# Closing an attention's output rows elsewhere in the schedule, and loading its keys through ScalarE's queue

## The chip, the core and the metric

The kernel runs on one core of a Trainium2 chip (trn2), in one launch. The metric is device time in microseconds, the median of several runs. Engines are named as in the profile: PE is TensorE's matmuls and PEld its weight loads, DVE is VectorE, ACT is ScalarE, POOL is GpSimd and SP is SyncE, which issues DMAs. Each engine takes its own instructions in program order.

## What is computed

The input x is (2, 2048, 512) in float32, with one condition vector per batch. Two layers follow each other. The first is a conditioned state-space block (norm and modulation, a diagonal scan along the length, a gate, a second norm, a feed-forward net 512 to 2048 to 512 with gelu, gated residuals). The second is an attention block; the change lies in it and just ahead of it:

```python
def _sln(h, w, ln_g, ln_b, Wg, bg, Wb, bb):
    mu = jnp.mean(h, axis=-1, keepdims=True)
    var = jnp.mean((h - mu) ** 2, axis=-1, keepdims=True)
    ln = (h - mu) / jnp.sqrt(var + EPS) * ln_g + ln_b
    gamma = (w @ Wg.T + bg)[:, None, :]
    beta = (w @ Wb.T + bb)[:, None, :]
    return gamma * ln + beta
...
h = _sln(hidden, w, ...)
q, k, v = (h @ Wqkv.T + bqkv) in 16 heads of 32
att = jax.nn.softmax(q @ k.T, axis=-1) / D ** 0.5
h1 = (att @ v) @ Wp.T + bp + hidden
h2 = _sln(h1, w, ...)
return h2 + h1
```

The last line is computed per row as y * g_row + (h1 + t_row), where y = (h1 - mean) * rstd, and g_row and t_row hold the condition's gamma and beta with ln_g and ln_b folded in.

## The kernel before

**Stages.** From 0 to about 1380 us the first layer runs over eight chunks of 512 rows (two batches of four), with the attention's norm, heads and values of the chunk before placed between. From 1380 to 1488 us lies the transition: at_norm (the attention's norm) of the last chunk, at_values of the last two chunks and at_heads of the last one, handed out from the list `left` (line 681), beside the first score work of the attention. In it, one PSUM bank (`ones`) serves all value tiles one after the other: at_values (line 541) does four matmuls into `pv`, DVE adds the bias row (line 548), which frees the bank, and SP stores the tile.

**Attention** runs from 1488 to 3513 us: 64 blocks, each a batch, a pair of heads and a chunk of 512 queries. A block has NP = 8 periods, numbered through j = 0 to 511. In each period 16 key tiles' worth of a block advances by two: ten tiles' scores are kept in SBUF 15 periods ahead (`keep`, lines 758 to 767: scores on PE, a copy on ACT, a running maximum on DVE), and six are made afresh in the period (`make`, 812 to 817: scores on PE, the shift added by DVE). `across` (769) takes the maximum of those six on PE and DVE. `turn_run` (785) turns the running maximum at positions 2 and 4 of a block's periods, and `spread` (795), at position 5, sends the negated maxima to DRAM (`flat`, 802) and reads them back on all partitions (`shift`, 804), for the block that begins three periods later. `take_off` (808, on POOL) adds the shift to kept scores a period ahead; `exponentials` (819, on ACT) run twice a period; `weighted` (824) multiplies the exponentials of the period before by the values.

**The order** is written out by hand: the loop at 1113 issues, for each j, first what `due` holds for j (run_due), then make, across, the first exponentials, the keeps, the pieces from `left`, the second exponentials, take_off for j + 1 and weighted for j - 1. Since every engine takes its instructions in this order, a place in the loop is a place in each engine's queue. `after(j, what, ...)` at 1055 enters a step. The schedule (1060 to 1103) enters, for block n: load_k (723, eight DMAs of 256 KB per pair of heads, i.e. per four blocks, at 8n - 27, which is position 5 of a block, the same due list as a spread and ahead of it), load_q (732, eight DMAs, position 3), load_v (742, two DMAs, 8n - 9).

**Closing the rows.** The output rows of a batch are closed in 16 tiles `qt` of 128 rows. Batch 0's are closed beside batch 1's attention, in blocks 34 to 57, a tile in every one and a half blocks, with all steps of a tile in fixed positions: last_rows (854) once, at block 34; then per tile fetch (874, six DMAs on SP) at position 3, divide (889, POOL) at position 5, project (894) in four groups at 6, 7, 0 and 1, moments (909, DVE) behind the last group, deviation (917, DVE, three Newton steps to 1/sqrt(var) in a PSUM tile `dev`) at the start of position 2, last_norm (937) at 3, close (946) at 4. last_norm has ACT write z = h * scale + shift to PSUM (941) and DVE multiply by g_row (943); close has POOL add t_row to h (949) and h to y (950), and SP store y (951). Twelve tiles of the last batch (LB) go through the same functions at the end (positions by `k = j + 3 + 2 * t`), and the last four rows' tiles through end_fetch to end_last (959 to 1027).

Of the kernel before, what the change touches and what calls it, by code (L numbers as in the profile page):

```python
# [8 lines left out]
F32 = mybir.dt.float32  # L9
# [4 lines left out]
AF = mybir.ActivationFunctionType  # L14
ALU = mybir.AluOpType
# [4 lines left out]
P = 128  # L20
# [19 lines left out]
def tile_s5_block_then_sln_attention(  # L40
# [21 lines left out]
    nc = tc.nc  # L62
    NB, L, D = x.shape
    KC = D // P
    CH = 512
# [4 lines left out]
    NG = D // P  # L70
# [5 lines left out]
    small = ctx.enter_context(tc.tile_pool(name="small", bufs=2))  # L76
# [26 lines left out]
    kd = [dpool.tile([2, D, L], F32, name=f"kd_{b}") for b in range(NB)]  # L103
# [98 lines left out]
    order = [(b, c) for b in range(NB) for c in range(NCH)]  # L202
# [59 lines left out]
    for q in range(4):  # L262
        f = FC // 4
# [58 lines left out]
    half, odd, turn, sign, even = col("half"), col("odd"), col("turn"), col("sign"), col("even")  # L322
# [64 lines left out]
    gate, last, bus, hs, pos, hids = {}, {}, {}, {}, {}, {}  # L387
# [127 lines left out]
    def at_norm(b, c):  # L515
        normalised(b, c)
        xc = xt.pop((b, c))
        for t in range(TT):
            nc.gpsimd.tensor_tensor(xc[:, t, :], xc[:, t, :], bp_row, ALU.add)
        nc.sync.dma_start(x2[b][c * CH : (c + 1) * CH, :].rearrange("(t p) d -> p t d", p=P), xc)  # L520
# [17 lines left out]
        nc.sync.dma_start(dst[0, g * P : (g + 1) * P, at], hi.bitcast(F32))  # L538
        nc.sync.dma_start(dst[1, g * P : (g + 1) * P, at], lo.bitcast(F32))

    def at_values(b, c, t):
        pv = ones.tile([P, CH], F32, name="pv")
        for k in range(KC):
            nc.tensor.matmul(
                pv, fts[b, c][:, k, t * P : (t + 1) * P], wv[:, k, :], start=k == 0, stop=k == KC - 1
            )
        vt = work1.tile([P, D], F32, name="vt", tag="gated")
        nc.vector.tensor_add(vt, pv, bv_row)
        nc.sync.dma_start(vd[b][c * CH + t * P : c * CH + (t + 1) * P, :], vt)


# [54 lines left out]
    for name, src in (("wk", w_kT), ("wq", w_qT), ("wv", w_vT)):  # L606
        w = wlate.tile([P, KC, D], F32, name=name)
# [3 lines left out]
    bv_row = wlate.tile([P, D], F32, name="bv_row")  # L611
# [14 lines left out]
    for i, now in enumerate(order):  # L626

        due = {(f, h): [] for f in range(FC + 1) for h in range(2)}
# [34 lines left out]
        def run_due(at):  # L663
            for what, *args in due[at]:
                what(*args)
# [15 lines left out]
    left = []  # L681
    for chunk in order[-2:]:
        for t in range(TT):
            left.append((at_values, *chunk, t))
    for j in range(2 * KC):
        left.insert(TT + j, (at_heads, *order[-1], j))
    for k in range(KC):
# [16 lines left out]
    ps = ctx.enter_context(tc.tile_pool(name="ps2", bufs=1, space=PSUM, side="right"))  # L704
# [6 lines left out]
    u, v = NPAIR - 2, NPAIR - 1  # L711
# [11 lines left out]
    def load_k(i):  # L723
        b, p = pairs[i]
        for e in range(2):
            f = slice(HD * (2 * p + e), HD * (2 * p + e + 1))
            ks = kpools[i % 2].tile([P, L], HALF, name="ks")
            for r in range(4):
                nc.sync.dma_start(ks[32 * r : 32 * r + 32, :].bitcast(F32), kd[b][r % 2, f, :])
            kst[i, e] = ks  # L730

    def load_q(n):
# [161 lines left out]
    def project(b, qt, groups=tuple(range(NG))):  # L894

        o4, h, *py = held[b, qt]
        if py:
            py = py[0]
        elif len(groups) == NG:
            py = ps.tile([P, 2, CH], F32, name="py2", tag="m")[:, 0, :]  # L900
        else:
            py = ps.tile([P, CH], F32, name="py", tag="pt")
        for g in groups:
            nc.tensor.matmul(py, o4[:, g, :], wp[:, g, :], start=g == 0, stop=g == NG - 1)
        held[b, qt] = o4, h, py
        if groups[-1] == NG - 1:
            held[b, qt] = h, moments(h, py)

    def moments(h, py):
        nc.vector.tensor_add(h, py, h)  # L910
        st = small.tile([P, 6], F32, name="st3")
        nc.vector.bn_stats(st, h)
        mv = small.tile([P, 2], F32, name="mv3", bufs=4)
        nc.vector.bn_aggr(mv, st)
        return mv

    def deviation(b, qt):

        h, mv = held[b, qt]
        w = ps.tile([P, 3], F32, name="dev", tag="pt")  # L920
        v, c = w[:, 0:1], w[:, 1:2]
        half = small.tile([P, 1], F32, name="half3")
        y = small.tile([P, 1], F32, name="scale3", bufs=3)
        nc.vector.tensor_scalar(v, mv[:, 1:2], EPS, None, ALU.add)
        nc.vector.tensor_scalar(half, v, -0.5, None, ALU.mult)
        nc.vector.tensor_scalar(
            y.bitcast(I32), v.bitcast(I32), -0.5, float(0x5F3759DF), ALU.mult, ALU.add
        )
        for _ in range(3):
            nc.vector.tensor_scalar(c, y, y, half, ALU.mult, ALU.mult)  # L930
            nc.vector.scalar_tensor_tensor(y, c, 1.5, y, ALU.add, ALU.mult)
        shift = small.tile([P, 1], F32, name="shift3", bufs=3)
        nc.vector.tensor_scalar(c, mv[:, 0:1], y, None, ALU.mult)
        nc.vector.tensor_scalar(shift, c, -1.0, None, ALU.mult)
        held[b, qt] = h, y, shift

    def last_norm(b, qt):

        h, scale, shift = held[b, qt]
        z = ps.tile([P, CH], F32, name="z", tag="pt")  # L940
        nc.scalar.activation(z, h, AF.Identity, bias=shift, scale=scale)
        y = work.tile([P, D], F32, name="y")
        nc.vector.tensor_tensor(y, z, ending[b][0], ALU.mult)  # L943
        held[b, qt] = h, y

    def close(b, qt):

        h, y = held.pop((b, qt))
        nc.gpsimd.tensor_tensor(h, h, ending[b][1], ALU.add)  # L949
        nc.gpsimd.tensor_tensor(y, y, h, ALU.add)  # L950
        nc.sync.dma_start(out[b, qt * P : (qt + 1) * P, :], y)


# [79 lines left out]
    AHEAD = 15  # L1033
# [18 lines left out]
    due = {}  # L1052

    def after(j, what, *args):
        due.setdefault(j, []).append((what, args))

    N = len(blocks)
    FIRST = -AHEAD - 8
    OPEN = -4
    for i, n in enumerate(opens):  # L1060
        free = NP * (max(m for m in range(N) if pair_of[m] == i - 2) + 1) if i > 1 else FIRST
        after(max(free, NP * n - AHEAD - 12), load_k, i)
        after(max(OPEN, NP * n - 9), load_v, i)
# [5 lines left out]
    for b in range(NB):  # L1069
        for c in range(NQ):  # L1070
            j = NP * (blocks.index((b, NPAIR - 1, c)) + 1) + 1
            if (b, c) == (LB, LC):
                most = slice(0, NH - 4)
                j = NP * (N - 1) - 2
                after(j - 3, fetch_sums, b, c, most)
                after(j - 1, invert, b, c, most)
                after(j + 1, end_fetch)
                after(NP * (N - 1) + 3, end_fetch_more)
                for g in range(NG - 1):
                    after(j + 5 + g, end_divide, g)  # L1080
                after(NP * N + 2, end_project, list(range(NG - 1)))
                after(NP * N + 20, end_last)
                continue
            after(j, fetch_sums, b, c)
            after(j + 2, invert, b, c)
            if c == 0:
                after(j + 2, last_rows, b) if b == LB else after(NP * (NPAIR * NQ * (b + 1) + 2), last_rows, b)
            for t in range(TT):
                qt = c * TT + t
                if b == LB:  # L1090
                    k = j + 3 + 2 * t
                    after(k + 3, project, b, qt)
                else:

                    k = NP * (NPAIR * NQ * (b + 1) + 2 + 3 * qt // 2) + 3
                    for g in range(NG):
                        after(k + 3 + g, project, b, qt, (g,))
                last = k + 3 if b == LB else k + 6
                after(k, fetch, b, qt)
                after(k + 2, divide, b, qt)  # L1100
                after(last + 1, deviation, b, qt)
                after(last + 2, last_norm, b, qt)
                after(last + 3, close, b, qt)

    def run_due(j):
        for what, args in due.pop(j, ()):
# [2 lines left out]
    def block_at(j):  # L1109
        n, i = divmod(j, NP)  # L1110
        return (n, i) if 0 <= n < N else (None, i)

    for j in range(FIRST, NP * N + 2):
# [27 lines left out]
        for kt in todo:  # L1141
            keep(n, kt)
        if j == -AHEAD - 1:
            at_norm(*order[-1])
            pieces = TT
        elif -AHEAD <= j < -AHEAD + 2:
            pieces = 2
        elif j >= -AHEAD + 2:
            pieces = -(-len(left) // (OPEN - j)) if j < OPEN else 0
        else:  # L1150
            pieces = 0
        for _ in range(pieces):
# [69 lines left out]
```

## Time and profile before

| | |
|---|---|
| median of 3 runs | 3555.16 us (3552.39 to 3559.92) |
| profiled execution | 3553.08 us |
| its span | 3551.2 us |
| PE busy | 3375.1 us, 95% |
| DVE busy | 2243.7 us, 63% |
| POOL busy | 1977.0 us, 56% |
| ACT busy | 1897.9 us, 53% |
| POOL take_off (line 810) | 640 of 2391 ns |
| ACT kept scores (line 762) | 640 of 1013 ns |
| DVE running maximum (line 767) | 512 of 1221 ns |

A share of busy time is a mean over all stages, and the stages differ: the first layer uses little but PE, the attention uses four engines. So the stretch in question is to be read by itself. A wait ("A <- B") is idle time of engine A that ended when B's instruction or DMA did; it costs nothing unless it is passed on to the engine that bounds. Times of DMA instructions on SP are those of their issue, not of the transfer.

### The profile page before, as it was taken

What the parts mean: (1) busy time and instruction counts of PE and PEld (TensorE: products, weight loads), DVE (VectorE), ACT (ScalarE), POOL (GpSimd) and SP (SyncE); (2) the same over time, 40 slices, a digit from 0 to 9 for tenths busy, and PEclk for the clock granted to TensorE, in tenths of its full rate; (3) what the DMA queues carried; (4) which work ended last, traced back from release to release, by engine and by line L of the source; (5) the groups of instructions that cost most, each with busy time, mean ns of one, the idle gap of its engine ahead of it and who ended that gap; (6) DMA issues with size and microseconds to landing.
All of it is one profiled execution on the core that took longest, in us unless ns stands there. A gap on an engine that the chain in (4) does not pass through costs nothing. (4 is left out here: it accounts for less than half of the span.)

```text
span 3551.2 us, 34223 instructions
## 1 busy us (share of the span) xinstructions
PE 3375.1 (95%) x11752; PEld 1531.9 (43%) x11752; DVE 2243.7 (63%) x3184; ACT 1897.9 (53%) x2143; POOL 1977.0 (56%) x1000
## 2 busy tenths in 40 slices
PE   7999999999999998899999999999999999999986
PEld 4444444444444443444444444444444444444432
DVE  6233232323222212589999999898888888988875
ACT  2111112111111111488888888888777877877853
POOL 4223131313131311288778888887777777777875
PEclk8999999999999999999999999999999999999998
DMA  8011111111101112412321222232323323323233
GB/s 296 1 36 39 45 42 48 36 48 36 54 33 39 36 45 74 119 47 64 76 69 49 71 65 70 49 75 61 87 67 81 82 69 77 76 72 88 59 94 98
DMA packets 201710, 237.07 MB, mean 67 GB/s; under 512 B 89857, under 2 KB 119041, under 8 KB 197441
## 3 DMA queue, kind: packets, MB, share of 16 engines
q1 hardware_dynamic: 201536, 234.89, 23.8%
q8 instruction: 93, 1.52, 0.2%
q14 instruction: 81, 0.66, 0.1%
HBM read 166.91 MB, written 67.76 MB: 66 GB/s over the span
## 5 line engine op out<-in xcount | busy, mean ns | idle before, releaser
L810 POOL TENSOR_TENSOR x<-x,shift 128x1024 f32<-128x1024 f32 x640 | 1505.1, 2391 | 284.1 <-DMA shift<-flat 237.6
L762 ACT COPY x<-s 128x1024 f32<-128x1024 f32 x640 | 635.2, 1013 | 297.7 <-PE s L751 294.2
L751 PE MATMUL s<-qs,ks 128*128 128x512 f32 x2048 | 699.5, 433 | 78.0 <-DVE run L767 55.9
L821 ACT ACTIVATE x<-x 128x1024 f32<-128x1024 f32 x640 | 676.4, 1057 | 42.8 <-POOL x L810 42.7
L767 DVE TENSOR_TENSOR run<-s,run 128x1024 f32<-128x1024 f32 x512 | 625.2, 1221 | 76.3 <-ACT x L762 57.4
L831 PE MATMUL o<-x,v 128*64 128x512 f32 x2560 | 669.5, 618 | 0.9 <-ACT x L821 0.9
L816 DVE TENSOR_TENSOR pT<-s,shift 128x1024 f32<-128x1024 f32 x384 | 467.4, 1217 | 49.8 <-PE s L751 44.2
L781 DVE TENSOR_REDUCE top<-m 128x1 f32<-128x768 f32 x512 | 485.9, 949 | 19.6 <-PE m L776 19.2
L751 PEld LDWEIGHTS s<-qs,ks 128*128 128x128 f32 x2048 | 347.4, 190 | 333.3 <-DVE run L767 144.7
L502 PE MATMUL po<-w_sb,hid 128*128 128x512 f32 x1024 | 460.3, 592 | 0.0
L489 PE MATMUL ph<-fT,w_sb 128*128 128x512 f32 x1024 | 459.7, 593 | 0.0
L821 ACT ACTIVATE pT<-pT 128x1024 f32<-128x1024 f32 x384 | 407.5, 1061 | 76.6 <-DVE pT L816 63.2
L493 ACT ACTIVATE hid<-ph,vec 128x512 f32<-128x512 f32 x128 | 88.0, 687 | 591.4 <-PE ph L489 591.4
L831 PE MATMUL o<-pT,v 128*64 128x512 f32 x1536 | 397.3, 596 | 4.6 <-ACT pT L821 4.6
L160 DVE SCALAR_TENSOR_TENSOR lo<-pk,vec,hi 128x512 fp32r<-128x512 f32 x64 | 48.0, 751 | 501.5 <-ACT hi L159 501.5
L776 PE MATMUL m<-ks,qs 128*128 128x384 f32 x1024 | 288.0, 362 | 7.0 <-DVE top L781 3.3
L489 PEld LDWEIGHTS ph<-fT,w_sb 128*128 128x128 f32 x1024 | 191.8, 190 | 226.5 <-issue 226.5
L502 PEld LDWEIGHTS po<-w_sb,hid 128*128 128x128 f32 x1024 | 191.1, 190 | 221.5 <-issue 221.5
L436 POOL TENSOR_TENSOR m<-m,m 128x512 f32<-128x512 f32 x8 | 13.1, 1643 | 442.1 <-DVE m L434 442.1
L159 ACT ACTIVATE hi<-pk,vec 128x512 fp32r<-128x512 f32 x64 | 44.0, 688 | 391.9 <-PE pk L532 391.9
L831 PEld LDWEIGHTS o<-x,v 128*64 128x64 f32 x2560 | 139.5, 136 | 263.6 <-issue 157.9
L512 POOL TENSOR_TENSOR x<-x,gated 128x512 f32<-128x512 f32 x32 | 39.6, 1271 | 349.5 <-DVE gated L511 349.5
(236 smaller groups left out, 2825.1 us busy)
## 6 DMA issues: line engine op xcount, KB each, us to landing
ks<-kd SPq DMA_DIRECT2D x128, 256.0 KB
qs<-qd SPq DMA_DIRECT2D x512, 64.0 KB
shift<-flat SPq DMA_DIRECT2D x64, 512.0 KB
x<-in_x SPq DMA_DIRECT2D x8, 1024.0 KB
w_sb<-in_w SPq DMA_DIRECT2D x8, 1024.0 KB
x<-x SPq DMA_DIRECT2D x8, 1024.0 KB
kd<-hi SPq DMA_DIRECT2D x32, 256.0 KB
kd<-lo SPq DMA_DIRECT2D x32, 256.0 KB
```

The lines of the kernel that those rows point to most:

```text
L489: nc.tensor.matmul(ph, w1_sb[:, k, f * P : (f + 1) * P], fts[b, c][:, k, :], start=k == 0, stop=k == KC - 1)
L493: nc.scalar.activation(hids[f], ph, AF.Gelu_apprx_tanh, bias=vec[:, V_B1 + f : V_B1 + f + 1], scale=1.0)
L502: nc.tensor.matmul(pos[b, c][:, t, :], hid[:, t * P : (t + 1) * P], w2_sb[:, f, :], start=f == 0, stop=f == FC - 1,)
L751: nc.tensor.matmul(s[:, e, :], kst[pair_of[n], e][:, kt * P : (kt + 1) * P], qst[n][:, e, :], start=True, stop=True,)
L762: nc.scalar.copy(x, s)
L767: nc.vector.tensor_tensor(runs[n], s, kept[n, 0] if kt == 1 else runs[n], ALU.max)
L776: nc.tensor.matmul(m[:, i, :YW], qst[n][:, e, t * P : (t + 1) * P], kst[pair_of[n], e][:, k : k + YW], start=True, stop=True,)
L781: nc.vector.tensor_reduce(tops[n][:, j, 0:1], m[:, :, :YW], AX.XY, ALU.max, negate=True)
L810: nc.gpsimd.tensor_tensor(x, x, shifts[n], ALU.add)
L816: nc.vector.tensor_tensor(x, s, shifts[n], ALU.add)
L821: nc.scalar.activation(x, x, AF.Exp)
L831: nc.tensor.matmul(outs[n][64 * e : 64 * e + 64, :], v[:, kt, e : e + 2, :], x[:, e, :], start=first, stop=final,)
```

## The change

It has six parts. (1) In the transition the values of the next to last chunk are copied out of PSUM by ACT and get their bias on POOL, and at_norm of the last chunk is issued behind them instead of ahead. (2) Keys are loaded by DMAs that ACT issues, not SP, and at 8n - 22 (position 2), not 8n - 27 (position 5); the first two loads move from j = -23 and 5 to -22 and 10. (3) The first pair's values are loaded at OPEN + 2, not OPEN. (4) A second due list (`closing`) runs behind the second exponentials of a period; moments and deviation of batch 0 go there (end of positions 1 and 2), deviation of batch 1 too. (5) deviation holds its columns in SBUF in ten instructions instead of twelve, last_norm has ACT write y to SBUF, and the product with g_row goes to POOL in close. (6) For batch 0, fetch comes at position 1 instead of 3, last_norm at 5, the addition of t_row to h by itself at 5 (into the freed tile o4), and close at 7; for batch 1 last_norm moves a period later, into the period of close.

```diff
-    def at_values(b, c, t):
+    def at_values(b, c, t, beside_norm=False):
...
-        nc.vector.tensor_add(vt, pv, bv_row)
+        if beside_norm:
+            nc.scalar.copy(vt, pv)
+            nc.gpsimd.tensor_tensor(vt, vt, bv_row, ALU.add)
+        else:
+            nc.vector.tensor_add(vt, pv, bv_row)
...
-            left.append((at_values, *chunk, t))
+            left.append((at_values, *chunk, t, chunk != order[-1]))
...
-                nc.sync.dma_start(ks[32 * r : 32 * r + 32, :].bitcast(F32), kd[b][r % 2, f, :])
+                nc.scalar.dma_start(ks[32 * r : 32 * r + 32, :].bitcast(F32), kd[b][r % 2, f, :])
...
-        if groups[-1] == NG - 1:
-            held[b, qt] = h, moments(h, py)
-
-    def moments(h, py):
+
+    def moments(b, qt):
+
+        o4, h, py = held[b, qt]
         nc.vector.tensor_add(h, py, h)
...
-        return mv
+        held[b, qt] = h, o4.rearrange("p g q -> p (g q)"), mv
+
+    def add_t(b, qt):
+        h, ht, *_ = held[b, qt]
+        nc.gpsimd.tensor_tensor(ht, h, ending[b][1], ALU.add)
 
     def deviation(b, qt):
...
-        w = ps.tile([P, 3], F32, name="dev", tag="pt")
-        v, c = w[:, 0:1], w[:, 1:2]
-        half = small.tile([P, 1], F32, name="half3")
+        v = small.tile([P, 1], F32, name="v3")
+        c = small.tile([P, 1], F32, name="c3")
         y = small.tile([P, 1], F32, name="scale3", bufs=3)
+        shift = small.tile([P, 1], F32, name="shift3", bufs=3)
         nc.vector.tensor_scalar(v, mv[:, 1:2], EPS, None, ALU.add)
-        nc.vector.tensor_scalar(half, v, -0.5, None, ALU.mult)
...
+        nc.vector.tensor_scalar(v, v, -0.5, None, ALU.mult)
         for _ in range(3):
-            nc.vector.tensor_scalar(c, y, y, half, ALU.mult, ALU.mult)
-            nc.vector.scalar_tensor_tensor(y, c, 1.5, y, ALU.add, ALU.mult)
-        shift = small.tile([P, 1], F32, name="shift3", bufs=3)
-        nc.vector.tensor_scalar(c, mv[:, 0:1], y, None, ALU.mult)
-        nc.vector.tensor_scalar(shift, c, -1.0, None, ALU.mult)
-        held[b, qt] = h, y, shift
+            nc.vector.tensor_scalar(c, y, y, v, ALU.mult, ALU.mult)
+            nc.vector.tensor_scalar(y, c, 1.5, y, ALU.add, ALU.mult)
+        nc.vector.tensor_scalar(shift, mv[:, 0:1], -1.0, y, ALU.mult, ALU.mult)
+        held[b, qt] = h, ht, y, shift
 
     def last_norm(b, qt):
...
-        z = ps.tile([P, CH], F32, name="z", tag="pt")
-        nc.scalar.activation(z, h, AF.Identity, bias=shift, scale=scale)
         y = work.tile([P, D], F32, name="y")
-        nc.vector.tensor_tensor(y, z, ending[b][0], ALU.mult)
+        nc.scalar.activation(y, h, AF.Identity, bias=shift, scale=scale)
...
     def close(b, qt):
 
-        h, y = held.pop((b, qt))
-        nc.gpsimd.tensor_tensor(h, h, ending[b][1], ALU.add)
-        nc.gpsimd.tensor_tensor(y, y, h, ALU.add)
+        h, ht, y = held.pop((b, qt))
+        if b == LB:
+            ht = h
+            nc.gpsimd.tensor_tensor(h, h, ending[b][1], ALU.add)
+        nc.gpsimd.tensor_tensor(y, y, ending[b][0], ALU.mult)
+        nc.gpsimd.tensor_tensor(y, y, ht, ALU.add)
...
+    def closing(j, what, *args):
+
+        due.setdefault(j + 0.5, []).append((what, args))
...
-        after(max(free, NP * n - AHEAD - 12), load_k, i)
-        after(max(OPEN, NP * n - 9), load_v, i)
+        after(max(free, NP * n - AHEAD - 7) if i > 1 else max(FIRST, NP * n - AHEAD - 7), load_k, i)
+        after(max(OPEN + 2, NP * n - 9), load_v, i)
...
+                    after(k + 3, moments, b, qt)
...
+                    closing(k + 6, moments, b, qt)
                 last = k + 3 if b == LB else k + 6
-                after(k, fetch, b, qt)
+                after(k if b == LB else k - 2, fetch, b, qt)
                 after(k + 2, divide, b, qt)
-                after(last + 1, deviation, b, qt)
-                after(last + 2, last_norm, b, qt)
-                after(last + 3, close, b, qt)
+                closing(last + 1, deviation, b, qt)
+                after(last + (3 if b == LB else 4), last_norm, b, qt)
+                after(last + (3 if b == LB else 6), close, b, qt)
+                if b != LB:
+                    after(last + 4, add_t, b, qt)
...
         if j == -AHEAD - 1:
-            at_norm(*order[-1])
             pieces = TT
...
+        if j == -AHEAD - 1:
+            at_norm(*order[-1])
         if now is not None:
             exponentials(now, uses[k][1])
+        run_due(j + 0.5)
```

More of the change, by code (lines that the diff above doesn't have):

```diff
@@ L914, in moments @@
         nc.vector.bn_aggr(mv, st)
-        return mv
+        held[b, qt] = h, o4.rearrange("p g q -> p (g q)"), mv
+    def add_t(b, qt):
+        h, ht, *_ = held[b, qt]
+        nc.gpsimd.tensor_tensor(ht, h, ending[b][1], ALU.add)
     def deviation(b, qt):
-        h, mv = held[b, qt]
-        w = ps.tile([P, 3], F32, name="dev", tag="pt")
-        v, c = w[:, 0:1], w[:, 1:2]
-        half = small.tile([P, 1], F32, name="half3")
+        h, ht, mv = held[b, qt]
+        v = small.tile([P, 1], F32, name="v3")
+        c = small.tile([P, 1], F32, name="c3")
         y = small.tile([P, 1], F32, name="scale3", bufs=3)
+        shift = small.tile([P, 1], F32, name="shift3", bufs=3)
         nc.vector.tensor_scalar(v, mv[:, 1:2], EPS, None, ALU.add)
-        nc.vector.tensor_scalar(half, v, -0.5, None, ALU.mult)
         nc.vector.tensor_scalar(
@@ L928, in deviation @@
         )
+        nc.vector.tensor_scalar(v, v, -0.5, None, ALU.mult)
         for _ in range(3):
-            nc.vector.tensor_scalar(c, y, y, half, ALU.mult, ALU.mult)
-            nc.vector.scalar_tensor_tensor(y, c, 1.5, y, ALU.add, ALU.mult)
-        shift = small.tile([P, 1], F32, name="shift3", bufs=3)
-        nc.vector.tensor_scalar(c, mv[:, 0:1], y, None, ALU.mult)
-        nc.vector.tensor_scalar(shift, c, -1.0, None, ALU.mult)
-        held[b, qt] = h, y, shift
+            nc.vector.tensor_scalar(c, y, y, v, ALU.mult, ALU.mult)
+            nc.vector.tensor_scalar(y, c, 1.5, y, ALU.add, ALU.mult)
+        nc.vector.tensor_scalar(shift, mv[:, 0:1], -1.0, y, ALU.mult, ALU.mult)
+        held[b, qt] = h, ht, y, shift
     def last_norm(b, qt):
-        h, scale, shift = held[b, qt]
-        z = ps.tile([P, CH], F32, name="z", tag="pt")
-        nc.scalar.activation(z, h, AF.Identity, bias=shift, scale=scale)
+        h, ht, scale, shift = held[b, qt]
         y = work.tile([P, D], F32, name="y")
-        nc.vector.tensor_tensor(y, z, ending[b][0], ALU.mult)
-        held[b, qt] = h, y
+        nc.scalar.activation(y, h, AF.Identity, bias=shift, scale=scale)
+        held[b, qt] = h, ht, y
     def close(b, qt):
-        h, y = held.pop((b, qt))
-        nc.gpsimd.tensor_tensor(h, h, ending[b][1], ALU.add)
-        nc.gpsimd.tensor_tensor(y, y, h, ALU.add)
+        h, ht, y = held.pop((b, qt))
[4 more added lines that the diff above has]
+        nc.gpsimd.tensor_tensor(y, y, ht, ALU.add)
         nc.sync.dma_start(out[b, qt * P : (qt + 1) * P, :], y)
```

## The prediction

> **What bounds the kernel now.** I read the busy shares of the page first, then busy time by stretches of 100 us (core us, then PE, PE's weight loads, DVE, ACT, POOL busy, clock, DMA share, GB/s):
>
> ```profile
> PE 3375.1 (95%) x11752; PEld 1531.9 (43%) x11752; DVE 2243.7 (63%) x3184; ACT 1897.9 (53%) x2143; POOL 1977.0 (56%) x1000
> ...
> 1400.00:1500.00 100.00, 80.54 (x231) 39.77 (x230) 49.94 (x55) 35.60 (x40) 12.71 (x8) 0.93 0.41 119
> 1700.00:1800.00 100.00, 98.17 (x424) 44.67 (x424) 90.69 (x92) 89.05 (x97) 84.74 (x37) 1.00 0.24 64
> 2700.00:2800.00 100.00, 91.86 (x373) 41.07 (x373) 84.39 (x107) 77.21 (x83) 78.04 (x36) 0.98 0.34 81
> 3400.00:3500.00 100.00, 84.37 (x282) 31.96 (x281) 70.14 (x170) 50.41 (x56) 79.45 (x47) 0.97 0.46 130
> ```
>
> TensorE bounds: nothing gains but what fills its gaps. It is full in attention's first half (98%), not in the transition (80%), the second half, where batch 0's rows are closed (92%), and the tail (84%). Next, the waits of blocks 33 to 57 (2440 to 3285 us), by engine and line: total us, times, longest.
>
> ```profile
> POOL x L810 <- DMA shift<-flat: 85.7, 19, 10.0
> POOL xr L949 <- ACT z L941: 63.5, 16, 5.3
> PEld s L751 <- DVE run L767: 62.6, 81, 5.3
> ...
> POOL o L891 <- DMA by<-invd: 38.6, 8, 9.3
> ```
>
> From the starts of the first exponentials (L821) a clean block takes 28.8 us, a period 3.6. These 25 blocks take 840.5, not 720. Batch 0's projections explain 64 x 0.853 = 54.6 us; 65.9 are stalls. Block by block: 23.5 at positions 0 to 2 of blocks 33, 37, 41, 45, 49 and 53 (1.4 to 5.65 each), 3.3 beside last_rows, 16 x 1.97 = 31.5 at positions 1 to 5 of a row tile's closing, 7.6 at positions 3 and 4 of five blocks where POOL sat on z. Block 37's start, SP's queue and POOL:
>
> ```profile
> 2563.63 0.36 SPq L951 DMA_DIRECT2D out<-y  x1
> 2564.03 3.68 SPq L729 DMA_DIRECT2D ks<-kd  x8
> 2568.26 0.27 SPq L802 DMA_DIRECT2D flat<-neg_row  x1
> 2576.05 0.34 SPq L804 DMA_DIRECT2D shift<-flat  x1
> ...
> 2580.40 4.66 POOL L810 TENSOR_TENSOR x<-x,shift 128x1024 f32<-128x1024 f32 x2 [9.75 <-DMA shift<-flat]
> ```
>
> Eight keys stand ahead of the 4 KB of flat. From flat to shift takes 7.8 us here, 1.06 without keys, and POOL starts 9.75 us late. The transition, where PE waits for the only bank left for values:
>
> ```profile
> 1394.52 0.68 DVE L548 TENSOR_TENSOR vt<-pv,bv_row 128x512 f32<-128x512 f32 x1
> ...
> 1395.26 5.51 PE L544 MATMUL pv<-wv,fT 128*128 128x512 f32 x8 [11.09 <-DVE vt L548]
> ```
>
> DVE had the norm of the last chunk (at_norm, 10 us) ahead of that add. Last, DVE's groups in blocks 33 to 57 (busy us, mean ns):
>
> ```profile
> L930 DVE TENSOR_SCALAR dev<-scale,half 128x1 f32<-128x1 f32 x48 | 13.5, 281 | 1.8
> L912 DVE BATCH_NORM_STATS2 st<-xr 128x6 f32<-128x512 f32 x16 | 11.1, 695 | 0.6
> L943 DVE TENSOR_TENSOR y<-z,g_row 128x512 f32<-128x512 f32 x16 | 10.9, 681 | 0.0
> L931 DVE SCALAR_TENSOR_TENSOR scale<-dev,scale 128x1 f32<-128x1 f32 x48 | 7.6, 158 | 1.7
> ```
>
> **What the Trainium skill says.** "DMA: Bandwidth & Descriptors", section "Issuing engines are not separate DMA queues": transfers of any issuing engine run on the same 16 DMA engines and interleave; other issuers save only sequencer time. "Queues, rings and completion order" there: a ring is taken in order, and a DMA engine takes turns between rings, packet by packet. Block 37 agrees with the order: the keys' 256 packets move from 2565.21 to 2575.22, flat's eight at 2574.40. No DMA of before is issued by ScalarE, so interleaving isn't shown. "GPSIMD Engine Reference", section "Elementwise — side-by-side cycle accounting": a two-input add on GpSimd takes 1.96 times VectorE's time; the trace has 1.28 us (L949) against 0.681 (L943).
>
> **Part by part.** Base: the profiled execution, 3553.1 us (span 3551.2 and 1.9 around it), 2.1 below the median.
>
> *Values before the norm.* The four adds are replaced by an ACT copy (nearest: ACT's Identity to SBUF at L1023, 0.80 us) and a POOL add (1.28), and at_norm moves behind all four tiles. Before, the values' matmuls end at 1410.5. After, from pv(0)'s end at 1384.2, three more tiles of 3.7 us with a copy of about 0.65 to 0.8 and a semaphore between: 1384.2 + 3 x (3.7 + 1.2) = 1398.9, call it 1399.2. DVE does the norm meanwhile, so xn is ready at 1394.6 as before. POOL's adds push L519 (5.5 us) back to about 1401; it feeds only x2, read much later. **-11.3**. Ends: 0, if PE then waits for xn or the first keys; -12.
>
> *Values of the first pair behind the first shift.* load_v at OPEN issues 2 DMAs (4096 packets, 1479.2 to 1484.0) ahead of flat: flat at 1480.00, shift only at 1483.45. Two periods later they come behind it: 3.45 - 1.06 = 2.4 and some landing, **-3.1**. They then land at about 1487, before the first weighted (1496.6). Ends -4, 0.
>
> *Keys earlier.* load_k goes from position 5 to position 2, three periods (11.2 us) ahead of spread. Issue to last packet took 11.2 us in block 37, so flat just clears them, and in another ring needn't stand behind them. Of 23.5 I leave 2.5: **-21**. Ends: -23.5, and 0 if the overlap persists. Load 1 moves later (j = 5 to 10) and is needed only from j = 17; load 0 moves one period later, cover about 10 us.
>
> *Keys in ACT's queue.* 8 issues by 0.46 us (3.68 on SP) precede position 2's exponentials and keep copy. ACT idles 0.4 us a period; its results lead their readers on PE by 2.1 us or more (exponentials to o) and 1.3 to 2.0 (a keep copy to the next use of its bank). If the issues overlap what is queued inside ACT, 0.9 to 1.8 us of delay are left, a PE stall of 0 to 0.3 for each of 15 loads: **+3**. Ends: 0; and 15 x 3.7 = +55 if each issue stands whole on the path. What waits behind them: the exponentials, then o matmuls, and the copy, then DVE's run.
>
> *Batch 0's norm on DVE.* y = z x g_row leaves (0.68 us a tile). The 12 column operations (2.40 us) become 10, but their price is the pointer operand, not PSUM: 281 ns with two pointers, 158 to 222 with fewer. The new L931 has a pointer and an immediate, the shift one operation: again about 2.4. Moments (0.68 + 0.70 + 0.18 = 1.56) go to the end of position 1, where DVE idles 1.28; deviation to the end of position 2, ahead of position 3's make, where there is no slack, so it stalls PE by about 2.3. Before, 2.6 of a clean tile's 3.1 us of DVE work stalled. Gain 0.3 x 16: **-5**. Ends: +16 (a us a tile if moments collide with turn_run), -31.
>
> *POOL.* Adding t_row apart and closing at position 7 ends the 63.5 us in which POOL sat on z, and with it the 7.6: **-6**. The product with g costs 1.28 on POOL, which is 80% busy: nothing in blocks 34 to 57. With cover gone it would be 16 x 1.28 = 20.5. Fetch (6 DMAs on SP) moves two periods ahead, past load_q's 8; POOL's 38.6 us on by shrink, but these waits show in no period's length: 0. ACT's Identity now writes SBUF, 0.80 for 0.77: 0.
>
> *Tail.* Block 61 takes 52.6 us on a chain of DVE and PE (DVE xr waits for PE py 24.4 us); deviation at the period's end falls under py: about 4 tiles x 1.8 = -7. In blocks 62 and 63 POOL is busy 33.9 of 40.6 and 37.4 of 43.1 us; 4 x 1.28 = 5.1 more in each, and the h add now waits for y: +8. **+1**. Ends -8, +10.
>
> Sum: -11.3 - 3.1 - 21 + 3 - 5 - 6 + 1 = -42.4, so 3510.7 on the profiled execution, **3512.8** on the median.
>
> **Rivals.**
> (a) *Slower: ScalarE's queue becomes the stall.* A full issue of 3.7 us or a full ring in ACT's stream, 15 times, at position 2. For: ACT is 89% busy, and SP was held 8.4 us in key issues at blocks 41 and 53. Against: the slack above, and that SP's ring held other transfers then. Without the +3 the rest gains 45.4, so it decides from 3.0 us a load. At 3.7 with +8 for POOL in the tail: -45.4 + 55 + 8 = +18, **3573**.
> (b) *Smaller: keys and shift still collide*, since they share the DMA engines, or the late stalls were only partly theirs. Keys bring -8 in place of -21, the norm +2, the tail +5: -42.4 + 13 + 7 + 4 = -18.4, **3537**. For: the 10 us of packets and 11.2 us of lead leave no margin.
> (c) *Larger: deviation is covered too*, as PE has scores queued when position 3 begins: a further 1.6 us x 16 = 26, **3487**. Against: DVE led PE by 0.05 us there.
> (d) *SBUF columns do nothing* by themselves: I hold this likely, and it is in the forecast; only their place counts.
>
> **How the numbers follow.** Forecast 3513 (3500 to 3525): 0.55. (b) 0.23, (c) 0.12, (a) 0.07, a balance near zero (half of the ACT stall) 0.03. The range leaves out (a), the balance and most of (c)'s far side: 3486 to 3542. A measurement here tells about 0.2%, 7 us. Faster 0.90, same 0.03, slower 0.07.
>
> **What would show it.** PE's gap before the second pv falls from 11.1 to about 1 us. From flat to shift about 1.1 us in blocks 33 to 53, and POOL's 85.7 on shift under 40. POOL's wait for z is gone. ACT's wait and PE's idle at position 2 of key blocks say what issues cost: above 1 us of PE idle a load I am wrong towards (a). Position 3 of closing blocks: still some 2 us long; if 3.4, (c). Blocks 62 and 63 longer by 4 each, or POOL wasn't their bound. Wrong altogether if the second half's blocks keep 33.6 us on average.

## The result, and the profile after

The changed kernel takes 3688.01 us (median of 4, 3684.23 to 3691.13) against 3555.88 (4 runs): ratio 1.0371, 95% interval 1.0353 to 1.0389. I forecast 3513 and a gain of 1.2%; it is 3.7% slower, outside the range and beyond the rival that ended slower.

The profiled execution spans 3685.2 us against 3551.2. Its page and busy time by stretches (columns as before):

```profile
PE 3408.0 (92%) x11752; PEld 1541.8 (42%) x11752; DVE 2224.7 (60%) x3124; ACT 1895.9 (51%) x2147; POOL 2010.6 (55%) x1032
```
```profile
1700.00:1800.00 100.00, 92.32 (x386) 41.06 (x385) 83.36 (x83) 82.66 (x91) 76.19 (x34) 0.97 0.22 59
2700.00:2800.00 100.00, 86.23 (x346) 38.55 (x346) 77.18 (x96) 71.05 (x78) 77.98 (x37) 0.94 0.34 82
3510.00:3610.00 100.00, 69.56 (x202) 25.60 (x199) 46.59 (x112) 36.84 (x42) 70.42 (x44) 0.85 0.37 107
```

In these windows PE lost 6 points in the first half of the attention, which held no closing at all, 6 in the second, and the tail grew. I cut the spans at the first exponential of blocks 0, 33, 58 and 61. The table also holds two experiments told below, e4_both and e6_keys_pos0:

| stretch, us | before | after | e4_both | e6_keys_pos0 |
|---|---|---|---|---|
| start to block 0 | 1490.7 | 1478.7 | 1482.9 | 1482.2 |
| blocks 0 to 32 | 956.1 | 1014.9 | 953.8 | 953.2 |
| blocks 33 to 57 | 838.2 | 885.4 | 811.7 | 802.5 |
| blocks 58 to 60 | 93.1 | 93.1 | 93.2 | 93.1 |
| block 61 to the end | 173.1 | 213.0 | 168.0 | 167.2 |

The transition gained about what was forecast. In the first half every block from 2 on takes 28.8 us but the key-loading ones; blocks 5, 9 and so on to 29 take 36.4 to 36.7. In the second half the loading blocks take 38 to 47 us, 6 to 15.5 more than a block of the same kind without a load. The waits of ACT in 1500 to 3380 us show a new line:

```profile
ACT x L766 <- PE s L755: 226.2, 382, 2.1
ACT x L825 <- DMA ks<-kd: 122.5, 13, 14.2
```

ACT stands still for 122.5 us where it loads keys. One load of the first half, ACT and its queue (ACTq), then SP:

```profile
1884.89 1.01 ACT L766 COPY x<-s 128x1024 f32<-128x1024 f32 x1 [0.16 <-PE s L755]
1885.18 0.89 ACTq L733 DMA_DIRECT2D ks<-kd  x2
1885.80 1.06 ACT L825 ACTIVATE pT<-pT 128x1024 f32<-128x1024 f32 x1
1890.76 2.82 ACTq L733 DMA_DIRECT2D ks<-kd  x6
1893.63 1.06 ACT L825 ACTIVATE x<-x 128x1024 f32<-128x1024 f32 x1 [6.77 <-DMA ks<-kd]
```
```profile
1884.36 0.77 SPq L853 DMA_DIRECT2D od<-raw  x2
1885.23 4.58 SPq L743 DMA_DIRECT2D qs<-qd  x8
```

The issues are not long: 3.7 us for eight, as I had said. But between the second and the third ACT waits 4.7 us, to 1890.76: load_q's second transfer, which SP issued at 1885.64, has landed at 1890.74. The built program says why, and the semaphores that the trace records agree. A semaphore is, as the trace records it, a counter that a finished transfer raises and that an instruction waits for. In this program each DMA signals the end of its transfer on one of eight semaphores, taken in turn over all DMAs whoever issues them, and is issued only when the last DMA on that semaphore has landed. For this load (semaphore, and what it waits for):

```
key 1  DMAHW4  load_q of an earlier block (SP)
key 2  DMAHW1  sd<-raw, just issued (SP)
key 3  DMAHW6  load_q of this moment (SP)
key 4  DMAHW7  load_q of this moment (SP)
key 5  DMAHW0  load_q of this moment (SP)
key 6  DMAHW1  key 2 (ACT)
key 7  DMAHW2  load_q of this moment (SP)
key 8  DMAHW3  load_q of this moment (SP)
```

In the second half by and xr of fetch stand there too, and a load's eight issues take up to 15.8 us. What stands behind them on ACT is late, the exponentials and the copy of the kept scores. PE feels it through the copy:

```profile
1895.62 1.22 DVE L771 TENSOR_TENSOR run<-s,x 128x1024 f32<-128x1024 f32 x1 [5.64 <-ACT x L766]
1896.90 1.22 PE L755 MATMUL s<-qs,ks 128*128 128x512 f32 x2 [5.49 <-DVE run L771]
```

DVE's running maximum waits for the copy, and PE's next scores wait for DVE to be done with their bank. From 1510 to 2440 us the wait of PE's score matmuls for the running maximum rose from 16.9 to 58.0 us; the o matmuls' weight loads waited no longer for exponentials than before (63.7 us against 66.5).

The tail has a second cause. POOL in two periods of block 62:

```profile
3555.64 1.27 POOL L955 TENSOR_TENSOR xr<-xr,t_row 128x512 f32<-128x512 f32 x1 [4.53 <-ACT y L947]
...
3559.42 1.26 POOL L895 TENSOR_TENSOR o<-o,by 128x512 f32<-128x512 f32 x1
3560.64 4.65 POOL L814 TENSOR_TENSOR x<-x,shift 128x1024 f32<-128x1024 f32 x2
3572.41 1.27 POOL L955 TENSOR_TENSOR xr<-xr,t_row 128x512 f32<-128x512 f32 x1 [7.12 <-ACT y L947]
```

and the waits of 3525 to 3632 us:

```profile
DVE xr L914 <- PE py L908: 51.6, 6, 10.5
ACT x L825 <- POOL x L814: 37.3, 7, 6.8
...
ACT pT L825 <- DVE pT L820: 32.9, 6, 6.5
PE py L908 <- POOL o L895: 30.6, 7, 4.8
POOL xr L955 <- ACT y L947: 30.0, 7, 7.1
```

Read in a circle they are one ring of waits: POOL's close waits for ACT's y; divide (L895) stands behind close; PE's projection waits for divide; DVE's moments for PE, and the pT tile stands behind them; ACT's exponential waits for pT, and the next y stands behind it. One turn takes 16.8 us (3555.64 to 3572.41), for two periods.

### The profile page after: what moved, and what is told of

Same layout as the page of the kernel before. It is cut to its first block, busy times and chain, and to the rows that moved or that the text cites. A ratio compares the mean times of both kernels' runs of the same rounds, so it can differ in the third digit from the quotient of the medians.

```text
span 3685.2 us, 34079 instructions
## 1 busy us (share of the span) xinstructions
PE 3408.0 (92%) x11752; PEld 1541.8 (42%) x11752; DVE 2224.7 (60%) x3124; ACT 1895.9 (51%) x2147; POOL 2010.6 (55%) x1032
## 4 chain that ended last, share of the span: by engine, by line
PE 67%; DVE 14%; ACT 7%; DMA 4%; issue 3%; POOL 2%; SPq 1%; ACTq 0%; DVEq 0%; POOLq 0%
PE o L835 14%; PE ph L489 12%; PE po L502 12%; PE s L755 9%; DVE run L771 8%; PE pk L532 6%; ACT x L766 4%; PE py L908 3%; PE pv L544 3%; PE m L780 2%; DMA qs<-qd 2%; ACT x L825 2%; ACT pT L825 1%; DVE pT L820 1%; PE pu L423 1%
## 5 line engine op out<-in xcount | busy, mean ns | idle before, releaser
L755 PE MATMUL s<-qs,ks 128*128 128x512 f32 x2048 | 707.0, 435 | 147.7 <-DVE run L771 103.2
L825 ACT ACTIVATE x<-x 128x1024 f32<-128x1024 f32 x640 | 676.3, 1057 | 191.4 <-DMA ks<-kd 122.5
L835 PE MATMUL o<-x,v 128*64 128x512 f32 x2560 | 678.0, 625 | 4.4 <-ACT x L825 4.4
L835 PE MATMUL o<-pT,v 128*64 128x512 f32 x1536 | 406.5, 608 | 2.5 <-ACT pT L825 2.5
L160 DVE SCALAR_TENSOR_TENSOR lo<-pk,vec,hi 128x512 fp32r<-128x512 f32 x64 | 48.1, 751 | 502.7 <-ACT hi L159 497.0
```

Source lines behind the costliest of these rows:

```text
L755: nc.tensor.matmul(s[:, e, :], kst[pair_of[n], e][:, kt * P : (kt + 1) * P], qst[n][:, e, :], start=True, stop=True,)
L835: nc.tensor.matmul(outs[n][64 * e : 64 * e + 64, :], v[:, kt, e : e + 2, :], x[:, e, :], start=first, stop=final,)
```

## The experiments

Each edit is against the kernel named. "Time" is the median, the ratio is against the kernel before on the same chip.

**The two causes apart and together (e1 to e4).** e1_keys_sp, against after:

```diff
-                nc.scalar.dma_start(ks[32 * r : 32 * r + 32, :].bitcast(F32), kd[b][r % 2, f, :])
+                nc.sync.dma_start(ks[32 * r : 32 * r + 32, :].bitcast(F32), kd[b][r % 2, f, :])
```

> The changed kernel with the keys issued by SP again, at the new time. Reading of the two traces: the 15 loads in the loop cost 61 us in blocks 1 to 29 (7.6 to 8.2 each) and 83 us in blocks 33 to 56 (6 to 15.5 each), since ACT stands still between the second and the third of its eight key issues. Theory Q (it is ACT's stream that is held; SP held as long costs nothing): about 3688 - 144 = 3544, blocks 5, 9 and so on back to 28.8 us, and no new wait for shift beyond 2 us a load. Rival T (the new time is at fault, the keys meet load_q at position 2 and 3 whoever issues them): 3680 to 3690, PE idle at position 1 of those blocks stays.

3558.83 us, ratio 1.0006 (0.9997 to 1.0015): 129 us back. Rival T falls; blocks 5 to 29 are at 28.8 us. The last 15 us of the expected 144 did not come. Blocks 37, 41, 49, 53 and 56 still lose 1 to 4.5 us (position 7 takes 8.7 us in block 37, not 4.2), and it is the same wait, now on SP. Its queue in block 37, and the row that flat sends:

```profile
2574.20 8.51 SPq L733 DMA_DIRECT2D ks<-kd  x8
2583.76 8.33 SPq L743 DMA_DIRECT2D qs<-qd  x8
2592.18 0.28 SPq L806 DMA_DIRECT2D flat<-neg_row  x1
2593.73 0.34 SPq L808 DMA_DIRECT2D shift<-flat  x1
```
```profile
2583.44 0.24 ACT L804 COPY neg_row<-pt_neg 8x128 f32<-8x128 f32 x1
```

The last two keys wait for by and xr of the fetch ahead, and load_q's eight wait for a key each. So flat is issued 8.5 us after its row is ready (5.2 to 8.5 us in these five blocks, at most 0.43 in the others from 33 to 57). From flat to shift it then takes 1.6 us.

e3_norm_early, against after; e4_both has this edit and e1's:

```diff
-                after(last + (3 if b == LB else 4), last_norm, b, qt)
+                after(last + (2 if b == LB else 4), last_norm, b, qt)
```

> The changed kernel with batch 1's last_norm at k + 5 as before, close at k + 6. Theory L (in blocks 61 to 63 last_norm and close in one period make a ring: POOL's close waits for ACT's y, divide stands behind close, PE's projection behind divide, DVE's moments behind PE, ACT's exponential and y behind DVE): POOL's wait for y (30 us in blocks 62 and 63) goes, these blocks return to about 45 and 45 us, about 3688 - 30 = 3658. Rival P (the product with g, 12 x 1.28 us on POOL, fills the tail): 3680 to 3690, POOL busy over 95% there.

3643.38 us, ratio 1.0241 (1.0226 to 1.0256): 45 us back. Block 61 falls from 53.1 to 44.9, 62 from 63.4 to 43.4, the rest from 96.5 to 79.9. The ring needed last_norm and close in one period; a period apart it is open. The product is still on POOL, so rival P falls.

> The changed kernel with both edits, keys on SP at the new time and batch 1's last_norm at k + 5. If the two costs lie in different stretches they add: 3688 - 144 - 30 = 3514, and below the kernel before by about 40. If the tail's ring has another cause, 3540.

3509.64 us, ratio 0.9865 (0.985 to 0.988). Costs of 129 and 45 singly, 178 together: they add, within some 4 us. The rest of the change gains 46 us, near the 45 of my sum without the term for ACT's queue, but in part by luck: by the table the transition gave 7.8 of 14.4 and blocks 33 to 57 gave 26.6 of 32, while the tail gained 5.1 where I had a loss of 1.

**What holds ACT (e2 and e5).** e2_before_keys_act is the kernel before with the one edit of e1 reversed: keys issued by ACT at the old time.

> The kernel before with one edit, the keys issued by ACT, at the old time. In the built program each DMA takes one of eight completion semaphores in turn and waits until the last DMA on that semaphore has landed; in the changed kernel the third to eighth key wait for load_q's DMAs of the same moment, here in the first half for load_q's of two periods earlier. Theory S (that semaphore wait is what holds ACT): in blocks 1 to 29 a load costs 0 to 1.5 us, in blocks 33 to 53, where the keys wait for fetches issued just before, 3 to 8; about 3556 + 8 x 1 + 7 x 5 - 10 = 3590. Rival I (eight issues in ACT's stream cost what they cost, wherever they stand): 7.6 us a load in the first half too, 3670 or more.

3624.95 us, ratio 1.0187 (1.0166 to 1.0207), between the two, and both halves missed what I expected. In blocks 4 to 29 a load costs 5.9 to 7.7 us, about what rival I had asked for; blocks 33 to 57 take 842.9, hardly more than before. So the time doesn't tell the theories apart here, and the trace must. A load of its first half, ACT, SP and POOL:

```profile
1639.48 0.91 ACTq L729 DMA_DIRECT2D ks<-kd  x2
1640.37 1.07 ACT L821 ACTIVATE x<-x 128x1024 f32<-128x1024 f32 x1
1640.43 2.32 ACTq L729 DMA_DIRECT2D ks<-kd  x5
1642.79 0.26 ACT L800 COPY neg_row<-pt_neg 8x128 f32<-8x128 f32 x1 [1.35 <-PE m L776]
```
```profile
1643.07 0.27 SPq L802 DMA_DIRECT2D flat<-neg_row  x1
1650.72 0.34 SPq L804 DMA_DIRECT2D shift<-flat  x1
```
```profile
1654.27 13.99 POOL L810 TENSOR_TENSOR x<-x,shift 128x1024 f32<-128x1024 f32 x6 [13.20 <-DMA shift<-flat]
```

The eight issues run through in 3.62 us and ACT idles 1.35: where the semaphores are free, issuing costs what I had priced, so rival I falls for the issue itself. That ACT's ring (its queue of issued transfers) was full is excluded too: here it takes eight, in the changed kernel it stopped after two, and went on when the semaphore came. What costs here is something else. The keys are issued 3.9 us ahead of flat; in the first half of the kernel before SP, running ahead of the other engines, had issued them 7.8 to 9.4 us ahead. So flat takes 7.7 us to its shift, not 2.5 to 4.2, and POOL waits 13.2 us: position 7 of that block takes 7.7 us and not 3.35, the block 33.9 and not 28.8, and the next 1.3 more. Another ring did not spare flat the keys: in block 37 of the kernel before, with 4.2 us of lead on the same ring, it took 7.8. Its eight packets of 512 bytes start from 1648.81 on, 5.7 us after the issue, among the last of the keys' packets (to 1649.96).

e5_q_earlier, against e3 (keys on ACT):

```diff
-        after(max(FIRST + 1 + n, NP * n - AHEAD - 6), load_q, n)
+        after(max(FIRST + 1 + n, NP * n - AHEAD - 9), load_q, n)
```

> Keys issued by ACT at position 2 and batch 1's last_norm at k + 5 (3643 us so far), with one more edit: load_q three periods earlier, at position 0. In the built program the eight keys of a first half load then stand behind the DMAs of the block's stored sums and outputs and of a load_q issued two periods before, on their completion semaphores. Theory S (ACT stands still because a key's semaphore is still owed by a load_q of the same moment): in blocks 5 to 29 the eight issues run in under 4.5 us, not 8.4, and the load costs 1 us or less, not 7.6; in blocks 33 to 56, where they stand behind a fetch of the period before, 4 to 10 remain; 3643 - 8 x 7 - 20 = 3567. Rival I (issuing itself, or the DMA engines' share, costs 7.6): 3635 to 3645.

3556.26 us, ratio 1.0005 (0.9996 to 1.0014), 87 us less than e3 for moving a transfer whose data no score matmul waited for. The load that corresponds to the one above:

```profile
1880.25 0.86 ACTq L733 DMA_DIRECT2D ks<-kd  x2
1880.87 1.06 ACT L825 ACTIVATE pT<-pT 128x1024 f32<-128x1024 f32 x1
1881.16 2.79 ACTq L733 DMA_DIRECT2D ks<-kd  x6
1884.00 1.06 ACT L825 ACTIVATE x<-x 128x1024 f32<-128x1024 f32 x1 [2.07 <-POOL x L814]
```

The gap of 4.7 us is gone, and blocks 13 to 25 take 29.8 us instead of 36.4: 1.0 a load is left (3.9 and 3.6 in blocks 5 and 9, 1.4 in 29). In the second half, where fetch stands in load_q's place, eight issues still take 8.8 to 9.6 us (3.7 in block 45, whose load has no fetch beside it) and blocks 37, 41, 53 and 56 take 40 to 41 us. Theory S holds.

**The keys' time (e6).** e6_keys_pos0, against e4:

```diff
-        after(max(free, NP * n - AHEAD - 7) if i > 1 else max(FIRST, NP * n - AHEAD - 7), load_k, i)
+        after(max(free, NP * n - AHEAD - 9) if i > 1 else max(FIRST, NP * n - AHEAD - 7), load_k, i)
```

> The version with keys on SP and last_norm early (3510 us), load_k two periods earlier, at position 0 (8n - 24). In that version blocks 37, 41, 49, 53 and 56 still lose 2 to 4 us at position 7, where the keys, issued behind a fetch, meet the shift of position 5. Theory C (a collision of transfers): at position 0 the keys go ahead of the fetch and are through 5 periods before flat; 5 x 3 = 15 us less, 3495. Rival: the fetch and load_q behind the keys then come late instead (POOL waits for by), 3508 to 3515.

3502.13 us, ratio 0.9853 (0.9834 to 0.9872). Blocks 33 to 57 fall from 811.7 to 802.5; no loading block stands out any more. Half of the 15 us that I expected came, and theory C had the wrong cause: in e4, as in e1, flat left SP 5.7 to 7.9 us after its row was ready in the five blocks and then took 1.6 to 2.2 us to its shift; in e6 it leaves within 0.03 us. SP's held queue went, not a meeting of transfers. This version beats both kernels, 1.5% under the kernel before.

**The terms that I had priced (e7 to e12).** e7_values_old, against e4: at_norm ahead of the values again and the bias on DVE.

```diff
-            left.append((at_values, *chunk, t, chunk != order[-1]))
+            left.append((at_values, *chunk, t))
...
         if j == -AHEAD - 1:
+            at_norm(*order[-1])
             pieces = TT
...
-        if j == -AHEAD - 1:
-            at_norm(*order[-1])
```

> The version with keys on SP and last_norm early (3510 us), with the transition as in the kernel before: at_norm ahead of the values, the bias added by DVE. By the prediction's term: 11.3 us more, 3521. By the start of the first block's exponentials, which lies 12.0 us earlier in the changed kernel but only 7.8 earlier in this version: 7 to 8 more, 3518. If the first block waits for something else: 3510.

3526.39 us, ratio 0.9922 (0.9899 to 0.9946): 16.8 us more than e4, beyond all three of my numbers. In the profiled executions, 14.1 apart, block 0 begins 10.5 us later than in e4, against the forecast 11.3; the other 3.6 lie in stretches that the edit doesn't touch, and their cause is open.

e8_old_columns, against e4:

```diff
-        v = small.tile([P, 1], F32, name="v3")
-        c = small.tile([P, 1], F32, name="c3")
+        w = ps.tile([P, 3], F32, name="dev", tag="pt")
+        v, c = w[:, 0:1], w[:, 1:2]
+        half = small.tile([P, 1], F32, name="half3")
...
+        nc.vector.tensor_scalar(half, v, -0.5, None, ALU.mult)
-            nc.vector.tensor_scalar(y, c, 1.5, y, ALU.add, ALU.mult)
+            nc.vector.scalar_tensor_tensor(y, c, 1.5, y, ALU.add, ALU.mult)
...
+        nc.vector.tensor_scalar(c, mv[:, 0:1], y, None, ALU.mult)
+        nc.vector.tensor_scalar(shift, c, -1.0, None, ALU.mult)
```

> The version with keys on SP and last_norm early (3510 us), with deviation's old arithmetic (twelve operations, columns in a PSUM tile) at its new place. Theory N (columns in SBUF save nothing, a pointer operand is the price and the place is what counts): 3508 to 3513, periods 3 and 4 of the closing blocks as long within 0.3 us. Rival: the columns are what saves, 0.4 us a tile in blocks 33 to 57 and more in the tail: 3517 or more.

3519.25 us, ratio 0.9902 (0.9882 to 0.9921), 9.6 us more than e4. Half of each theory. In the closing blocks the old arithmetic, eleven operations and not the twelve that I had counted, is as quick (position 3: 5.19 us, in e4 5.25). But from block 61 to the end it takes 7.4 us more; block 61 takes 50.7 us, not 44.9: the columns are a tile of the PSUM buffer that py and spread's transpose share, and in blocks 61 and 62 (3338 to 3440 us) PE waits for it:

```profile
PE pt_neg L802 <- DVE shift L942: 5.0, 2, 3.9
```

The columns in SBUF save no DVE time here; they free a bank.

e9_front, against e6: moments and deviation of batch 0 at the starts of positions 1 and 2.

```diff
-                    closing(k + 6, moments, b, qt)
+                    after(k + 6, moments, b, qt)
...
-                closing(last + 1, deviation, b, qt)
+                (closing if b == LB else after)(last + 1, deviation, b, qt)
```

> The version with keys on SP at position 0 and last_norm early (3502 us), with batch 0's moments and deviation at the starts of positions 1 and 2, as in the kernel before (its columns stay in SBUF). By the prediction's term the closing at the ends of periods is worth 0.3 us a tile: 5 us more, 3507. By the blocks: a closing block of before with two thirds of a tile takes 34.2 and 32.5 us, of this version 33.8 and 32.0: 0.65 a tile, 10 in all, but the product is gone from DVE either way: 3503 to 3508. If the place is worth nothing: 3502.

3513.41 us, ratio 0.9876 (0.9861 to 0.989). Blocks 33 to 57 take 813.8, 11.3 more: the place is worth 0.7 us a tile, twice my 0.3.

e11_close_early, against e6: last_norm at 3 and close at 4 again.

```diff
-                after(last + (2 if b == LB else 4), last_norm, b, qt)
-                after(last + (3 if b == LB else 6), close, b, qt)
+                after(last + 2, last_norm, b, qt)
+                after(last + 3, close, b, qt)
                 if b != LB:
-                    after(last + 4, add_t, b, qt)
+                    after(last + 2, add_t, b, qt)
```

> The same version (3502 us), with batch 0's last_norm at position 3 and close at position 4 as in the kernel before (t_row is still added apart, at position 3). By the prediction's term, POOL sits on ACT's y for 3 to 5 us a tile as in the kernel before (63.5 us in all) and this costs 6 us: 3508. If POOL's wait is covered: 3502.

3517.99 us, ratio 0.9894 (0.9877 to 0.991), 15.9 us more; blocks 33 to 57 take 823.9, 21.4 more (block 0 began 4.3 earlier). The size was wrong and so was the engine. In 2480 to 3255 us:

```profile
ACT y L947 <- DVE shift L940: 47.6, 16, 3.0
```

With deviation at the end of position 2, a last_norm at 3 holds ACT 3 us a tile with the exponentials behind it. e6 has no such line; its POOL waits 42.0 us for y at position 7 and loses nothing. So the later last_norm is what makes the later deviation possible.

e12_fetch_late, against e6:

```diff
-                after(k if b == LB else k - 2, fetch, b, qt)
+                after(k, fetch, b, qt)
```

> The same version (3502 us), with batch 0's fetch at position 3 as in the kernel before. POOL then waits for by again, 2 to 9 us every other tile (38.6 in the kernel before). By the prediction this shows in no period: 3502 +-2. If the earlier fetch is part of the gain in blocks 33 to 57: 3508 or more.

3499.18 us, ratio 0.9837 (0.9823 to 0.9852), as e6. POOL waits for by 67.8 us, in e6 13.2, and blocks 33 to 57 take 803.1 against 802.5: covered.

e10_product_dve, against e6:

```diff
-        nc.gpsimd.tensor_tensor(y, y, ending[b][0], ALU.mult)
+        (nc.vector if b == LB else nc.gpsimd).tensor_tensor(y, y, ending[b][0], ALU.mult)
```

> The version with keys on SP at position 0 and last_norm early (3502 us), with the product with g of the last batch alone back on DVE. In blocks 62 and 63 of that version POOL is busy 42.7 of 43.0 and 39.7 of 40.0 us. Theory P (POOL bounds these two blocks, and 4 x 1.28 us a block of it are the product): 8 to 10 us less, 3493. Rival D (DVE, which waits for the projection and makes the pT tiles, takes them into its own chain: 8 x 0.69): 3500 to 3505.

3507.03 us, ratio 0.9859 (0.9845 to 0.9874): no gain. In the traces block 61 takes 48.1 us against 44.9, block 62 44.0 against 43.3. POOL, freed of the product, is busy 38.1 of 44.0 us in block 62 and waits, and DVE has the product in its own chain. Rival D holds. Whether POOL alone bounded block 62 in e6, busy 42.7 of 43.0 us, this run doesn't tell, since DVE got what POOL lost.

## Why the prediction was wrong

**The step that failed: "Keys in ACT's queue ... +3. Ends: 0; and 15 x 3.7 = +55".** I priced the issue alone. Its 3.7 us were right, and the slack around it nearly (e2: ACT idles 1.35; e5: 1.0 us a load in blocks 13 to 25, where I had allowed 0 to 0.3). What I left out is that a DMA instruction of this program is a wait: it stands until its completion semaphore is free, and that is owed by whatever transfer used it last, on SP's queue and in SP's time. On SP the wait holds other DMAs; on ACT it holds exponentials and score copies, and through the copies PE. It cost 8 us a load in the first half and 6 to 15.5 in the second: 61 + 83 = 144 by the blocks, 129 by e1. Rival (a) had the place right, but asked for the wrong thing ("a full issue of 3.7 us or a full ring"), and its 55 us was no upper bound. The trace of before did show the wait, in two of the loads. I had seen the one of block 41 (and that of block 53, 8.5 us):

```profile
2693.61 8.73 SPq L729 DMA_DIRECT2D ks<-kd  x8
```

and put it down to other transfers in SP's ring. SP's own waits from 1500 to 3500 us name the transfers of a fetch:

```profile
SPq L729 <- DMA by<-invd: 3.1, 2, 1.8
...
SPq L729 <- DMA xr<-x: 1.8, 2, 0.9
```

They are about half of what these two loads took beyond 3.7 us each. Most of the rest lies in each load's third issue, of 2.9 to 3.0 us, and its cause is open. In the other loads of the attention SP's issues ran through.

**The tail: "+1. Ends -8, +10".** 40 us in place of that (173.1 to 213.0). I saw that close would wait for y and added 8 for it, with the product. I did not follow what stands behind close on POOL (divide) round to y itself. Without the ring of waits (e4) the tail is 168.0, 5 under before. There block 61 takes 7.7 us less and block 62 takes 2.8 more, not the 4 of my sign; no run isolates what the product has in that.

**Values before the norm, -11.3: right, within a few us.** PE's gap before the second tile fell from 11.09 us to

```profile
1385.99 3.70 PE L544 MATMUL pv<-wv,fT 128*128 128x512 f32 x8 [1.76 <-ACT vt L549]
...
1394.84 3.70 PE L544 MATMUL pv<-wv,fT 128*128 128x512 f32 x8 [0.72 <-ACT vt L549]
```

and the values end at 1398.5 (1399.2 forecast). Block 0 begins 12.0 us earlier, e7 gives 10.5; the versions with the same transition, e5 with its moved load_q aside, begin it between 1477.9 and 1484.1 us. Of the 3.1 for the first pair's values no run isolates anything.

**Keys earlier, -21: the mechanism right, the place not enough.** From flat to shift the loads of the second half took 5.9 to 7.8 us before and at most 2.5 in e4. But with the keys on SP 12 us stayed (e1 814.5, e6 802.5), through SP's held issues; two periods more were needed in the half with fetches. My sign that POOL's wait for shift would fall under 40 us was not met: it is 91.8 in e4 and 67.8 in e6, and in e6 it is covered. That ACT's ring would let flat by was wrong (e2: 7.7 us to the shift). I had counted on turns short enough to let flat by. The Trainium skill, "DMA: Bandwidth & Descriptors", section "Queues, rings and completion order", says that a DMA engine drains a whole packet of a ring, typically about 9 to 17 descriptors (orders to move one piece), before it switches. If each 8 KB transfer in the trace, 585 ns in the mean, is one descriptor, a turn takes by estimate, from the page's 9 to 17 and this trace's 585 ns, 5.3 to 9.9 us. So flat's 5.7 us do not contradict the page; whether they were one turn no run shows.

**Norm and POOL, -5 and -6: right in sum, wrong in parts.** With the keys' terms these made 32 us for blocks 33 to 57 (838.2 us before; I had read 840.5). e4, with the keys at the forecast time, gained 26.6, and e6 35.7. The place of moments and deviation is worth 11.3, not 5; position 3 of a closing block is 1.9 us longer than a clean one, as I had said. POOL's wait for z was no cost by itself: it remains (42.0 us in e6) and is covered, and my sign that it would be gone was wrong. The prices of the column operations held: L938 273 ns, L939 214 ns, as estimated from before. My sign of being wrong altogether, that these blocks keep 33.6 us on average, came true through the keys: 35.4 in the changed kernel, 32.5 in e4.

**SBUF columns (d):** right for the arithmetic, wrong for the tail, where the bank counts (e8).

## What to carry to other kernels

Before a DMA is moved to a computing engine's queue, read which semaphore it waits on and which transfer owes it: the engine stops until that other transfer has landed, and its own work stops with it. A queue that nobody computes on can be held the same way, and what it carries for others then leaves late (flat in e1 and e4). Where a step is put a period later, follow what stands behind it on each engine until the circle closes or doesn't; two steps in one period can tie four engines into a ring that a period between them opens. When several edits come together, undo them one by one: here two of six hid a gain of 1.3% under a loss of 3.7%.

## What the runs showed that I had not expected

A transfer of 4 KB issued on SP began 5.7 us after its issue, when nearly all of the 2 MB on another engine's ring had gone (e2). Moving a load whose data no score matmul waited for by three periods changed the time by 87 us (e5), about half of it in the first half, where the keys' semaphores came free. An engine busy 42.7 of 43.0 us, relieved of four instructions of 1.28 us, did not make its block shorter, since they went to another engine of the same chain (e10).
